# Two residual blocks gather their neighbours by indirect transfers with an add, instead of by multiplying with a neighbour matrix

## The chip, the cores and the metric

The kernel runs on one core of one Trainium2 chip. The metric is the device time of one execution in microseconds (us). Engines are named as in the profile: PE is TensorE, DVE is VectorE, ACT is ScalarE, POOL is GpSimd, and SP is the queue that issues the plain DMA transfers. PEld is the loading of weights into TensorE. Each engine works through its own instructions in the order in which they stand in the program, and waits for the others through semaphores.

## The reference, cut to what matters

There are B = 4 independent batches. For each, a mixture of low-rank experts (L0) and a cross-attention with a layer norm (L1) give `points`, 256 channels by 512 points. Then come two layers (L2 and L3) of four residual blocks each, eight blocks per batch and 32 in all. They run one after the other within a batch:

```python
idx = top_k(-squared_distance(xyz), 8)            # 8 nearest of 512 points, once per batch
for i in range(4):                                # in L2, and again in L3
    shortcut = points                             # (256 channels, 512 points)
    p = where(points >= 0, points, 0.01 * points)
    g = p gathered at idx                         # 8 neighbours of each point
    c = w_center[i] @ p
    gn = w_neighbor[i] @ g
    points = (c + gn.sum(over the 8 neighbours)) / 9 + shortcut
```

Both weights are the same matrix W here, so a block needs W p once, and then for each point the sum of nine columns of it: its own and those of its eight neighbours. The neighbours depend on `ctx_4096` alone, so a batch has one list of them for all its blocks.

## The kernel before, in words

Arrays lie with 128 partitions. A batch's x is two tiles of 128 channels by 512 points.

**A residual block** is `block(b, i)`. DVE makes p (L857). PE multiplies it with W in two halves of 256 points; this gives (W p) transposed, points on the partitions, in PSUM tiles `wp` (L869). The gather is a second product: `nbr[b, m]` is a matrix of zeros and ones that says which points are neighbours of which, with the identity added. As ones and zeros are exact in PE's shorter float format but W p is not, ACT writes a rounded copy `wph` (L882), DVE the rest `wpl` (L885), and both are multiplied by `nbr` into the two PSUM tiles `blk` (L900), 16 products of 128x128 by 128x512 in a block. DVE divides by 9 and adds x (L912). The next block of this batch needs that x, so within a batch the blocks are one chain, and PE is kept at work by changing between batches.

**What goes ahead of the blocks in a batch**: `mixture` (L392 to L489; `upd` at L448 reads the weights `lora_BT`), `values`, `queries` and `attention` (L632 to L844), with a layer norm that ends in two POOL instructions (L843 and L844), and `nearest`, which finds the eight neighbours with DVE's `max` and `match_replace` (L532, L535), makes `near` on ACT, and turns it on PE (L556) into `nbr`.

**The order** is not written by hand. `Plan.add` records each operation with an engine and a written cost; `Plan.emit` then walks through time with these costs, takes on each engine the operation that can start first, and among those that can start within 0.05 us of it the one with the lowest rank. The rank is the batch's due time from `DEADLINES` less the length of the chain that hangs on the operation. What comes out is one fixed order per engine.

Of the kernel before, what the change touches and what calls it, by code (L numbers as in the profile page):

```python
# [8 lines left out]
F32 = mybir.dt.float32  # L9
# [15 lines left out]
NL = S // 128  # L25
NBLK = 4
KNN = 8
# [1 line left out]
SLOPE = 0.01  # L29
LN_EPS = 1e-5  # L30
LOW = -3.0e38
DEADLINES = (0.0, 5.0, 15.0, 20.0)

# [2 lines left out]


EARLY = {"PE": 0.0, "ACT": 0.09, "DVE": 0.08, "POOL": 0.02, "SP": 0.0}  # L40
WARM = 20
LANES = 8
RATE = 0.3
# [16 lines left out]
class Plan:  # L60
# [5 lines left out]

    def __init__(self, places, make):
        self.places = {k: [(0.0, i) for i in range(n)] for k, n in places.items()}  # L70
        self.make, self.ops, self.wrote, self.read = make, [], {}, {}
        self.batch, self.unit, self.landed = 0, None, [0.0] * LANES

    def add(self, eng, cost, fn, ins=(), outs=(), rank=None, load=0.0, port=None):
        op = Op()
        op.port = eng == "POOL" if port is None else port
        op.eng, op.cost, op.fn, op.rank, op.load = eng, cost, fn, rank, load
        op.batch, op.unit, op.n, op.before, op.after, op.end = self.batch, self.unit, len(self.ops), set(), [], None
        for k in ins:
            if k in self.wrote:  # L80
                op.before.add(self.wrote[k])
            self.read.setdefault(k, []).append(op)
        for k in outs:
            op.before.update(self.read.pop(k, []))
            if k in self.wrote:
                op.before.add(self.wrote[k])
            self.wrote[k] = op
        op.before.discard(op)
        op.bufs = [k for k in dict.fromkeys([*ins, *outs]) if isinstance(k, Buf)]
        for k in op.bufs:  # L90
            k.users.append(op)
        for o in op.before:
            o.after.append(op)
        self.ops.append(op)

    def emit(self, deadline):
        longest = {}
        for op in reversed(self.ops):
            op.tail = op.cost + max(
                [o.tail + (SEEN[op.eng] if o.eng != op.eng else 0.0) for o in op.after if o.batch == op.batch],  # L100
                default=0.0,
            )
            if op.unit:
                longest[op.unit] = max(longest.get(op.unit, 0.0), op.tail)
            op.todo = len(op.before)
            for k in op.bufs:
                k.left = len(k.users)
        for op in self.ops:
            if op.rank is None:
                op.rank = deadline[op.batch] - longest.get(op.unit, op.tail)  # L110
        free, port = dict.fromkeys(SEEN, 0.0), {"POOL": 0.0, "DVE": 0.0}
        ready = [op for op in self.ops if not op.todo]
        while ready:
            best = {}
            for op in ready:
                t = free[op.eng] if not op.load else max(free[op.eng], self.landed[-LANES])
                if op.port:
                    t = max(t, port["DVE"] + 0.06 if op.eng == "POOL" else port["POOL"])
                t = max([t] + [o.end + (SEEN[o.eng] if o.eng != op.eng else 0.0) for o in op.before])
                want = {}  # L120
                for k in op.bufs:
                    if k.tile is None:
                        for kind in k.kinds:
                            want[kind] = want.get(kind, 0) + 1
                if any(len(self.places[kind]) < n for kind, n in want.items()):
                    continue
                for kind, n in want.items():
                    t = max(t, sorted(self.places[kind])[n - 1][0])
                best.setdefault(op.eng, []).append((t, op))
            choice = []  # L130
            for eng, found in best.items():
                first = min(t for t, _ in found)
                t, op = min((f for f in found if f[0] <= first + 0.05), key=lambda f: (f[1].rank, f[1].n))
                choice.append((t, op.n, op))
            t, _, op = min(choice)
            ready.remove(op)
            for k in op.bufs:
                if k.tile is None:
                    k.held = []
                    for kind in k.kinds:  # L140
                        self.places[kind].sort()
                        k.held.append(self.places[kind].pop(0)[1])
                    k.tile = self.make(k.kinds[0], k.held[0], k.name)
            op.fn()
            op.end = t + op.cost
            free[op.eng] = op.end - (EARLY[op.eng] if op.cost > 0.3 else 0.0)
            if op.port:
                port[op.eng] = free[op.eng]
            if op.load:
                op.end = max(op.end + 1.4, self.landed[-1]) + op.load / RATE  # L150
# [14 lines left out]
def xattn_seq_kernel(ctx: ExitStack, tc: tile.TileContext, a: dict, out: bass.AP):  # L165
# [5 lines left out]
    work = ctx.enter_context(tc.tile_pool(name="work", bufs=1))  # L171
    small = ctx.enter_context(tc.tile_pool(name="small", bufs=1))
    psum = ctx.enter_context(tc.tile_pool(name="psum", bufs=1, space=bass.MemoryType.PSUM))
    ctx.enter_context(tc.manual_schedule())

    shapes = {
# [5 lines left out]
        "full": (work, [128, 2, H], F32, 4),  # L182
        "wp": (work, [128, 2 * S], F32R, 8),
        "near": (work, [128, H], BF16, 5),
        "odd": (work, [128, H], U8, 2),
        "small": (small, [128, 4 * NB], F32, 12),
    }
# [17 lines left out]
    csq = [keep.tile([128, H], F32R, name=f"csq{b}") for b in range(B)]  # L205
    cxx = [keep.tile([128, H], F32, name=f"cxx{b}") for b in range(B)]
    WkT = [keep.tile([128, H], F32, name=f"WkT{c}") for c in range(NC)]
    nbr = {}
    nbr_tag = [
        [f"nbr0_{k}" for k in range(4)],  # L210
        [f"WkT{k}" for k in range(4)],
# [29 lines left out]

    mbias = const.tile([128, B, V], BF16, name="mbias")
    some = const.tile([128, B], F32, name="some")


    loads = []
# [22 lines left out]
    def load_points(b):  # L269
# [39 lines left out]
        rank=-1e4,  # L309
# [26 lines left out]
        ("hsel",),  # L336
        ("hsel2",),
    )
    pool(0.1, lambda: G_.memset(eps, LN_EPS), (), ("eps",), port=False)
    pool(0.1, lambda: G_.memset(above, 1.0 + LOW * 2.0**-123), (), ("above",), port=False)  # L340
    for k in range(2):
# [90 lines left out]
    def mix(b, l, zb):  # L432
# [11 lines left out]
        for h in range(2):  # L444
            pe(
                1.73,
                lambda h=h: [
                    T_.matmul(  # L448
                        ps2.tile,
                        lhsT=zT.tile[:, bass.ts(c, 128)],  # L450
                        rhs=w["lora_BT"][:, c, :],
                        start=(c == 0),
                        stop=(c == NC - 1),
                    )
                    for c in (2 * h, 2 * h + 1)
                ],
                (zT, "lora_BT"),
                (ps2,),
            )
        key = ("x", b, l)  # L460
        dve(
# [30 lines left out]
    def nearest(b):  # L492
# [36 lines left out]
        for j in range(H // 128):  # L529
# [16 lines left out]
                (near,),  # L546
            )
            nears.append(near)
        for k in range(H // 128):

            ps = Buf("bank", f"nbrT{b}_{k}", "stage")
# [297 lines left out]


    def block(b, i):
        pt, wi = x1[b], fT[:, i % NBLK]
        p = Buf("full", f"p{b}_{i}")
        for l in range(NL):
            dve(
# [3 lines left out]
                (("p", b, l),),  # L859
                port=True,  # L860
            )
        parts = []
        for m2 in range(2):
            ps = Buf("bank", f"wp{b}_{i}_{m2}")
            hi, lo = Buf("wp", f"wph{b}_{i}_{m2}"), Buf("wp", f"wpl{b}_{i}_{m2}")
            pe(
                1.73,
                lambda ps=ps, m2=m2: [
                    T_.matmul(  # L869
                        ps.tile[:, bass.ts(k, S)],  # L870
                        lhsT=p.tile[:, c, bass.ts(2 * m2 + k, 128)],
                        rhs=wi[:, c, :],
                        start=(c == 0),
                        stop=(c == NL - 1),
                    )
                    for k in range(2)
                    for c in range(NL)
                ],
                (("p", b, 0), ("p", b, 1), p, "fT"),
                (ps, hi, lo),  # L880
            )
            act(0.59, lambda ps=ps, hi=hi: A_.copy(hi.tile, ps.tile), (ps,), (hi,))  # L882
            dve(
                0.69,
# [9 lines left out]
        for m2 in range(2):  # L894
            for o in range(NL):
# [10 lines left out]
                            )  # L906

                pe(0.92, gather, (*parts[m2], ("nbr", b, 2 * m2), ("nbr", b, 2 * m2 + 1)), (pb[o],))
        for o in range(NL):
            dve(  # L910
                0.69,
# [80 lines left out]
```

## Time and profile before

| what | value |
|---|---|
| median of 3 runs | 406.25 us (405.9 to 406.34) |
| the profiled execution's own time | 406.27 us |
| its span in the profile | 404.5 us, so 1.8 us lie around the span |
| PE busy | 398.3 us, 98% of the span |
| DVE, ACT, POOL busy | 264.7, 130.4 and 93.0 us |
| granted TensorE clock | 0.998 of full speed |

The span is what the profile covers, from the first to the last thing that it records. A group of instructions in the profile stands for one source line, engine, operation and shape; it has the busy time, the mean of one, and how long the engine sat idle just before. Matmuls overlap each other in PE's pipeline, so the mean of one record is longer than what one adds to the time; what a run of them takes is read from the chain, where each piece has a start and a length.

### The profile page before, as it was taken

How to read it: one execution, taken by the hardware profiler on the slowest of the kernel's cores; microseconds unless marked ns; L12 is line 12 of the kernel's file. 1: busy time of each engine (PE TensorE's matmuls, PEld its weight loads, DVE VectorE, ACT ScalarE, POOL GpSimd, SP SyncE). 2: the span in 40 equal slices, each digit the busy share in tenths (PEclk: the TensorE clock that was granted, in tenths of full speed). 3: DMA queues.
4: the chain of work that ended last, by engine and by line, in shares of the span. 5: the costliest groups of instructions: out<-in, count | busy, mean ns of one | idle time of the engine just before them, and what ended most of it. 6: DMA issues, size and time to landing. Idle time of an engine off the chain costs nothing.

```text
span 404.5 us, 5757 instructions
## 1 busy us (share of the span) xinstructions
PE 398.3 (98%) x2324; PEld 306.6 (76%) x2324; DVE 264.7 (65%) x476; ACT 130.4 (32%) x234; POOL 93.0 (23%) x94
## 2 busy tenths in 40 slices
PE   8999999999999999999999999999999999999996
PEld 6755786656857767866778888888888888888884
DVE  3855659997999999745588644646455463635433
ACT  4652153555464485131244222111111111111110
POOL 4644320727945808605000000000000000000000
PEclk9999999999999999999999999999999999999999
DMA  6995100000000000000000000000000000010102
GB/s 229 364 421 210 52 2 0 2 2 0 2 2 0 2 2 1 2 2 0 0 0 2 0 2 0 0 2 0 2 0 1 2 0 0 2 52 1 53 0 104
DMA packets 4746, 15.33 MB, mean 38 GB/s; under 512 B 688, under 2 KB 816, under 8 KB 4080
## 3 DMA queue, kind: packets, MB, share of 16 engines
q1 hardware_dynamic: 4720, 14.97, 9.9%
q8 instruction: 18, 0.29, 0.3%
q14 instruction: 8, 0.07, 0.1%
HBM read 12.87 MB, written 2.10 MB: 37 GB/s over the span
## 4 chain that ended last, share of the span: by engine, by line
PE 98%; DVE 1%; ACT 0%; issue 0%
PE blk L900 29%; PE wp L869 27%; PE upd L448 7%; PE o L818 7%; PE q L670 7%; PE pT L786 3%; PE d L512 3%; PE avT L798 2%; PE v L632 2%; PE route L392 2%; PE s L711 2%; PE kT L578 2%; PE d L525 1%; PE zT L438 1%; PE nbrT L556 1%; PE x1T L477 1%
## 5 line engine op out<-in xcount | busy, mean ns | idle before, releaser
L869 PE MATMUL wp<-fT,p 128*128 128x256 f32 x512 | 119.0, 380 | 0.0
L900 PE MATMUL blk<-nbr,wph 128*128 128x512 f32 x256 | 109.8, 429 | 0.0
L869 PEld LDWEIGHTS wp<-fT,p 128*128 128x128 f32 x512 | 96.6, 189 | 16.8 <-issue 1.2
L900 PE MATMUL blk<-nbr,wpl 128*128 128x512 f32 x256 | 100.6, 393 | 0.9 <-DVE wpl L885 0.9
L912 DVE SCALAR_TENSOR_TENSOR x<-blk,x 128x512 f32<-128x512 f32 x64 | 43.8, 687 | 76.9 <-PE blk L900 76.9
L882 ACT CAST wph<-wp 128x512 fp32r<-128x512 f32 x64 | 37.6, 587 | 168.4 <-PE wp L869 168.4
L885 DVE TENSOR_TENSOR wpl<-wp,wph 128x512 fp32r<-128x512 f32 x64 | 44.0, 687 | 24.5 <-ACT wph L882 24.5
L900 PEld LDWEIGHTS blk<-nbr,wpl 128*128 128x128 f32 x256 | 48.2, 188 | 11.4 <-DVE wpl L885 1.6
L900 PEld LDWEIGHTS blk<-nbr,wph 128*128 128x128 f32 x256 | 48.2, 188 | 11.3 <-ACT wph L882 0.8
L857 DVE SCALAR_TENSOR_TENSOR p<-x 128x512 f32<-128x512 f32 x64 | 44.8, 732 | 0.4
L774 POOL TENSOR_TENSOR s<-s,rden 128x512 f32<-128x512 f32 x32 | 35.1, 1132 | 36.4 <-DVE rden L764 35.6
L818 PE MATMUL o<-WoT,avTs 128*128 128x512 f32 x64 | 29.6, 597 | 0.0
L448 PE MATMUL upd<-lora_BT,zTs 128*128 128x512 f32 x64 | 29.2, 600 | 0.0
L670 PE MATMUL q<-x1T,WqT 128*128 128x256 f32 x128 | 28.7, 380 | 0.0
L670 PEld LDWEIGHTS q<-x1T,WqT 128*128 128x128 f32 x128 | 23.9, 190 | 3.5 <-issue 0.5
L737 DVE TENSOR_REDUCE mx<-s 128x8 f32<-128x512 f32 x32 | 19.9, 684 | 4.9 <-PE s L711 4.8
L448 PEld LDWEIGHTS upd<-lora_BT,zTs 128*128 128x128 f32 x64 | 11.6, 190 | 12.5 <-issue 11.8
L743 DVE TENSOR_TENSOR s<-s,mx 128x512 f32<-128x512 f32 x32 | 20.1, 684 | 0.0
L752 DVE TENSOR_REDUCE den<-s 128x8 f32<-128x512 f32 x32 | 19.9, 679 | 0.2
L818 PEld LDWEIGHTS o<-WoT,avTs 128*128 128x128 f32 x64 | 11.4, 190 | 10.6 <-issue 10.4
L749 ACT ACTIVATE s<-s 128x512 f32<-128x512 f32 x32 | 18.8, 633 | 1.8 <-DVE s L743 1.6
L791 ACT COPY pTs<-pT 128x512 f32<-128x512 f32 x32 | 17.0, 597 | 7.1 <-PE pT L786 7.1
(97 smaller groups left out, 376.7 us busy)
## 6 DMA issues: line engine op xcount, KB each, us to landing
xT<-in_xT SPq DMA_DIRECT2D x4, 512.0 KB, 6.7
x<-in_x SPq DMA_DIRECT2D x4, 512.0 KB, 12.2
out<-x SPq DMA_DIRECT2D x8, 256.0 KB, 2.0
WkT<-in_WkT SPq DMA_DIRECT2D x4, 256.0 KB, 7.7
lora_BT<-in_lora_BT SPq DMA_DIRECT2D x1, 1024.0 KB, 7.9
WqT<-in_WqT SPq DMA_DIRECT2D x1, 1024.0 KB, 9.9
WvT<-in_WvT SPq DMA_DIRECT2D x1, 1024.0 KB, 11.0
rows<-in_rows SPq DMA_DIRECT2D x2, 512.0 KB, 12.0
```

What stands on the lines that cost most here:

```text
L448: T_.matmul(ps2.tile, lhsT=zT.tile[:, bass.ts(c, 128)], rhs=w["lora_BT"][:, c, :], start=(c == 0), stop=(c == NC - 1),)
L670: T_.matmul(ps.tile[:, 0:S], lhsT=w["WqT"][:, c, bass.ts(o, 128)], rhs=x1T[b].tile[:, c, :], start=(c == 0), stop=(c == NC - 1),)
L737: lambda mx=mx, ps=ps: V_.tensor_reduce(mx.tile[:, 0:HPC], heads(ps), AX.X, ALU.max),
L743: lambda mx=mx, ps=ps, s=s: V_.tensor_tensor(heads(s), heads(ps), mx.tile[:, 0:HPC].unsqueeze(2).to_broadcast([128, HPC, V]), ALU.subtract),
L774: lambda s=s, g=g: G_.tensor_tensor(heads(s), heads(s), rden.tile[:, bass.ts(g, HPC)].unsqueeze(2).to_broadcast([128, HPC, V]), ALU.mult,),
L818: T_.matmul(po.tile, lhsT=avT.tile[:, bass.ts(c, 128)], rhs=w["WoT"][:, c, :], start=(c == 0), stop=(c == NC - 1),)
L857: lambda l=l: V_.scalar_tensor_tensor(p.tile[:, l], pt[:, l], SLOPE, pt[:, l], ALU.mult, ALU.max),
L869: T_.matmul(ps.tile[:, bass.ts(k, S)], lhsT=p.tile[:, c, bass.ts(2 * m2 + k, 128)], rhs=wi[:, c, :], start=(c == 0), stop=(c == NL - 1),)
L882: act(0.59, lambda ps=ps, hi=hi: A_.copy(hi.tile, ps.tile), (ps,), (hi,))
L885: lambda ps=ps, hi=hi, lo=lo: V_.tensor_tensor(lo.tile, ps.tile, hi.tile.bitcast(F32), ALU.subtract),
L900: T_.matmul(pb[o].tile, lhsT=part.tile[:, bass.ds(m % 2 * S + o * 128, 128)], rhs=nbr[b, m], start=(m == 0 and k == 0), stop=(m == H // 12 ...
L912: lambda o=o: V_.scalar_tensor_tensor(pt[:, o], pb[o].tile, 1.0 / (KNN + 1.0), pt[:, o], ALU.mult, ALU.add),
```

## The change

In blocks 3 and 5 of batch 3 (`APART`) the gather isn't a product any more. W p goes by ACT to an SBUF tile `sums` (points on partitions, in place of `lora_BT`, which is dead by then), and from there by one plain transfer of 512 KB to a DRAM tile `rows`. Then 32 indirect transfers are issued from POOL: for each of the eight neighbours k and each of the four groups t of 128 points, one transfer fetches 128 rows of 1 KB from `rows`, chosen by the list `listed`, and adds them to the rows of `sums` where they lie. Those of one group form a chain of eight, each waiting for the one before; four chains go side by side. At the end PE turns `sums` back in 8 transposes, and DVE adds it to x as before. In these blocks the copies `wph` and `wpl` go.

For the list, batch 3's `nearest` gets, four times, a POOL product of `near` with the numbers 1 to 512, a DVE `max` that pulls the eight numbers out, and a DVE subtraction of 1. The numbers are made once by POOL (`iota` and a copy).

The planner learns of a transfer's landing by a new term `late`, its tie window of 0.05 us goes, and the due times are others. So the whole order is planned anew.

```diff
-DEADLINES = (0.0, 5.0, 15.0, 20.0)
+DEADLINES = (20.0, 24.0, 40.0, 35.0)
+APART = ((3, 3), (3, 5))
...
-                t, op = min((f for f in found if f[0] <= first + 0.05), key=lambda f: (f[1].rank, f[1].n))
+                t, op = min((f for f in found if f[0] <= first), key=lambda f: (f[1].rank, f[1].n))
...
-            op.end = t + op.cost
-            free[op.eng] = op.end - (EARLY[op.eng] if op.cost > 0.3 else 0.0)
+            op.end = t + op.cost + op.late
+            free[op.eng] = t + op.cost - (EARLY[op.eng] if op.cost > 0.3 else 0.0)
...
+            if b in listed:
+                which, best = Buf("half", f"which{b}_{j}"), Buf("small", f"best{b}_{j}")
+                pool(1.3, lambda ...: G_.tensor_tensor(which.tile, near.tile, count, ALU.mult), (near, "count"), (which,))
+                dve(0.69, lambda ...: V_.max(best.tile[:, 0:KNN], which.tile), (which,), (best,))
+                dve(0.16, lambda ...: V_.tensor_scalar(listed[b][:, bass.ts(j, KNN)], best.tile[:, 0:KNN], -1.0, None, ALU.add), (best,), (("listed", b, j),))
...
+        if (b, i) in APART:
+            return apart(b, i, p)
...
+    def apart(b, i, p):
+        rows, tiles, n = Buf("rows", f"rows{b}_{i}"), range(H // 128), APART.index((b, i))
+        gone = [("upd", k, l, h) for k in range(B) for l in range(NL) for h in range(2)]
+        def total():
+            if not sums:
+                sums.append(keep.tile([128, 2, H // 128, S], F32, tag="lora_BT", name="sums"))
+            return sums[0][:, n % 2]
+        for m2 in range(2):
+            ps = Buf("bank", f"wp{b}_{i}_{m2}")
+            product(b, i, p, m2, ps, ())
+            act(0.59, lambda ps=ps, m2=m2: A_.copy(total()[:, 2 * m2 : 2 * m2 + 2, :].rearrange("p k o -> p (k o)"), ps.tile),
+                (ps, *gone), (("sum", n % 2, m2), *(("sum", n % 2, m2, k) for k in range(2))))
+        plan.add("SP", 0.45, lambda: S_.dma_start(out=rows.tile.rearrange("(t p) o -> p t o", p=128), in_=total()),
+            (("sum", n % 2, 0), ("sum", n % 2, 1)),
+            (rows, *(("sum", n % 2, t // 2, t % 2) for t in tiles)), late=4.5)
+        for k in range(KNN):
+            for t in tiles:
+                pool(1.2,
+                    lambda k=k, t=t: G_.indirect_dma_start(
+                        out=total()[:, t, :], out_offset=None, in_=rows.tile,
+                        in_offset=bass.IndirectOffsetOnAxis(ap=listed[b][:, t * KNN + k : t * KNN + k + 1], axis=0),
+                        compute_op=ALU.add),
+                    (rows, ("listed", b, t)), (("sum", n % 2, t // 2, t % 2),), port=False, late=3.0)
+        pb = [Buf("bank", f"blk{b}_{i}_{o}") for o in range(NL)]
+        for o in range(NL):
+            pe(0.48,
+                lambda o=o: [T_.transpose(pb[o].tile[:, bass.ts(t, 128)], total()[:, t, bass.ts(o, 128)], ident) for t in tiles],
+                ("ident", *(("sum", n % 2, t // 2, t % 2) for t in tiles)), (pb[o],))
+        update(b, i, pb)
```

`product` and `update` are the old product (L869) and the old last step (L912), made into functions.

More of the change, by code (lines that the diff above doesn't have):

```diff
@@ L72, in __init__, with add @@
         self.batch, self.unit, self.landed = 0, None, [0.0] * LANES
-    def add(self, eng, cost, fn, ins=(), outs=(), rank=None, load=0.0, port=None):
+    def add(self, eng, cost, fn, ins=(), outs=(), rank=None, load=0.0, port=None, late=0.0):
         op = Op()
+        op.late = late
         op.port = eng == "POOL" if port is None else port
@@ L98, in emit @@
         for op in reversed(self.ops):
-            op.tail = op.cost + max(
+            op.tail = op.cost + op.late + max(
                 [o.tail + (SEEN[op.eng] if o.eng != op.eng else 0.0) for o in op.after if o.batch == op.batch],
@@ L173, in xattn_seq_kernel @@
     psum = ctx.enter_context(tc.tile_pool(name="psum", bufs=1, space=bass.MemoryType.PSUM))
+    dram = ctx.enter_context(tc.tile_pool(name="dram", bufs=1, space=bass.MemoryType.DRAM))
     ctx.enter_context(tc.manual_schedule())
@@ L184, in xattn_seq_kernel @@
         "near": (work, [128, H], BF16, 5),
+        "rows": (dram, [H, S], F32, 1),
         "odd": (work, [128, H], U8, 2),
@@ L207, in xattn_seq_kernel @@
     WkT = [keep.tile([128, H], F32, name=f"WkT{c}") for c in range(NC)]
-    nbr = {}
+    nbr, sums = {}, []
     nbr_tag = [
@@ L243, in xattn_seq_kernel @@
     some = const.tile([128, B], F32, name="some")
+    count = const.tile([128, H], F32, name="count")
+    listed = {b: const.tile([128, H // 128 * KNN], I32, name=f"listed{b}") for b in {b for b, _ in APART}}
     loads = []
@@ L338, in xattn_seq_kernel @@
     )
+    steps = Buf("half", "steps")
+    pool(
+        0.7,
+        lambda: G_.iota(steps.tile.bitcast(I32), pattern=[[1, H]], base=1, channel_multiplier=0),
+        (),
+        (steps,),
+        port=False,
+    )
+    pool(0.6, lambda: G_.tensor_copy(count, steps.tile.bitcast(I32)), (steps,), ("count",))
     pool(0.1, lambda: G_.memset(eps, LN_EPS), (), ("eps",), port=False)
@@ L457, in mix @@
                 (zT, "lora_BT"),
-                (ps2,),
+                (ps2, ("upd", b, l, h)),
             )
@@ L548, in nearest @@
             nears.append(near)
+            if b in listed:
+                which, best = Buf("half", f"which{b}_{j}"), Buf("small", f"best{b}_{j}")
+                pool(
+                    1.3,
+                    lambda near=near, which=which: G_.tensor_tensor(which.tile, near.tile, count, ALU.mult),
+                    (near, "count"),
+                    (which,),
+                )
+                dve(0.69, lambda which=which, best=best: V_.max(best.tile[:, 0:KNN], which.tile), (which,), (best,))
+                dve(
+                    0.16,
+                    lambda best=best, j=j: V_.tensor_scalar(
+                        listed[b][:, bass.ts(j, KNN)], best.tile[:, 0:KNN], -1.0, None, ALU.add
+                    ),
+                    (best,),
+                    (("listed", b, j),),
+                )
         for k in range(H // 128):
@@ L851, in block @@
     def block(b, i):
-        pt, wi = x1[b], fT[:, i % NBLK]
+        pt = x1[b]
         p = Buf("full", f"p{b}_{i}")
@@ L865, in block @@
             hi, lo = Buf("wp", f"wph{b}_{i}_{m2}"), Buf("wp", f"wpl{b}_{i}_{m2}")
[L866 to L881, printed above, removed]
+            product(b, i, p, m2, ps, (hi, lo))
             act(0.59, lambda ps=ps, hi=hi: A_.copy(hi.tile, ps.tile), (ps,), (hi,))
@@ L908, in block, with product @@
                 pe(0.92, gather, (*parts[m2], ("nbr", b, 2 * m2), ("nbr", b, 2 * m2 + 1)), (pb[o],))
+        update(b, i, pb)
+    def product(b, i, p, m2, ps, outs):
+        pe(
+            1.73,
+            lambda: [
+                T_.matmul(
+                    ps.tile[:, bass.ts(k, S)],
+                    lhsT=p.tile[:, c, bass.ts(2 * m2 + k, 128)],
+                    rhs=fT[:, i % NBLK, c, :],
+                    start=(c == 0),
+                    stop=(c == NL - 1),
+                )
+                for k in range(2)
+                for c in range(NL)
+            ],
+            (("p", b, 0), ("p", b, 1), p, "fT"),
+            (ps, *outs),
+        )
@@ new lines, in apart @@
+    def apart(b, i, p):
[8 more added lines that the diff above has]
+            product(b, i, p, m2, ps, ())
+            act(
+                0.59,
+                lambda ps=ps, m2=m2: A_.copy(
+                    total()[:, 2 * m2 : 2 * m2 + 2, :].rearrange("p k o -> p (k o)"), ps.tile
+                ),
+                (ps, *gone),
+                (("sum", n % 2, m2), *(("sum", n % 2, m2, k) for k in range(2))),
+            )
+        plan.add(
+            "SP",
+            0.45,
+            lambda: S_.dma_start(out=rows.tile.rearrange("(t p) o -> p t o", p=128), in_=total()),
+            (("sum", n % 2, 0), ("sum", n % 2, 1)),
+            (rows, *(("sum", n % 2, t // 2, t % 2) for t in tiles)),
+            late=4.5,
+        )
+        for k in range(KNN):
+            for t in tiles:
+                pool(
+                    1.2,
+                    lambda k=k, t=t: G_.indirect_dma_start(
+                        out=total()[:, t, :],
+                        out_offset=None,
+                        in_=rows.tile,
+                        in_offset=bass.IndirectOffsetOnAxis(ap=listed[b][:, t * KNN + k : t * KNN + k + 1], axis=0),
+                        compute_op=ALU.add,
+                    ),
+                    (rows, ("listed", b, t)),
+                    (("sum", n % 2, t // 2, t % 2),),
+                    port=False,
+                    late=3.0,
+                )
+        pb = [Buf("bank", f"blk{b}_{i}_{o}") for o in range(NL)]
+        for o in range(NL):
+            pe(
+                0.48,
+                lambda o=o: [
+                    T_.transpose(pb[o].tile[:, bass.ts(t, 128)], total()[:, t, bass.ts(o, 128)], ident)
+                    for t in tiles
+                ],
+                ("ident", *(("sum", n % 2, t // 2, t % 2) for t in tiles)),
+                (pb[o],),
+            )
+        update(b, i, pb)
@@ L909, in block, with update @@
+    def update(b, i, pb):
+        pt = x1[b]
         for o in range(NL):
```

## The prediction

> **What bounds the kernel now.** I read the page's first two parts, then the chain of waits in order of time, then the groups by shape, then windows.
>
> ```profile
> PE 398.3 (98%) x2324; PEld 306.6 (76%) x2324; DVE 264.7 (65%) x476; ACT 130.4 (32%) x234; POOL 93.0 (23%) x94
> PEclk9999999999999999999999999999999999999999
> POOL 4644320727945808605000000000000000000000
> ```
>
> PE has no free time and runs at full clock; POOL has nothing to do in the second half. The chain (start, length, work) shows what a block costs PE:
>
> ```profile
> 359.39 1.73 PE wp L869 x8
> 361.12 1.86 PE blk L900 x8
> 362.98 1.73 PE wp L869 x8
> 364.70 1.85 PE blk L900 x8
> ...
> 97.85 1.31 PE pT L786 x12
> ...
> 396.92 3.74 PE blk L900 x16
> 400.66 0.02 issue
> 400.69 0.69 DVE x L912
> ```
>
> From 275 us to 400.7 it is wp and blk end to end with no gap: a block is 2 x 1.73 for W p and 2 x 1.855 = 3.71 for the gather, 7.17 in all. Here the time is PE's work, so PE work taken out comes off the time, if what replaces it is never waited for. Transposes of this kind (128x128) take 1.31/12 = 0.109 each.
>
> ```profile
> 0.00:40.00 40.00, 38.90 (x203) 25.53 (x204) 23.00 (x57) 19.31 (x35) 19.89 (x33) 1.00 0.82 310
> 80.00:120.00 40.00, 39.67 (x373) 26.37 (x372) 37.45 (x67) 22.09 (x40) 24.62 (x21) 1.00 0.01 2
> 120.00:160.00 40.00, 39.10 (x326) 28.55 (x325) 38.45 (x70) 23.24 (x42) 20.91 (x19) 1.00 0.00 1
> 280.00:320.00 40.00, 40.00 (x180) 33.73 (x179) 22.42 (x36) 6.46 (x11) 0.00 (x0) 1.00 0.00 1
> ```
>
> The columns after the length are PE, PEld, DVE, ACT, POOL, clock, DMA share and GB/s. From 80 to 160 us DVE is nearly as full as PE (37.5 and 38.5 of 40): attention is where DVE could become the bound. From 280 on it is half idle.
>
> **What is removed.** Two gathers, 2 x 3.71 = 7.42 of PE, put back as 2 x 8 transposes, 16 x 0.109 = 1.74. Net 5.7 off PE. Also 4 DVE subtractions go (L885, 0.687 each, 2.7). ACT keeps its four copies: another destination, the same 0.59.
>
> **What is added, beside PE.** POOL: four products `which` (as L471, 1.37 each) and the numbers, some 7 in all; DVE: four `max` of 0.69 and four small ones of 0.16, 3.4. They run in the first 60 us, before DVE is full: by 10 us slices DVE idles 25 of the first 60 us. The four `which` stand in POOL's listing between the additions L471 and L489 of batches 0 and 1, each of which can be held 1.4; PE has other batches' work there, so I count nothing; without that cover the worst is 4 x 1.4 = 5.6.
>
> **The transfers.** Before has no transfer issued by POOL and none that adds. Three prices are needed.
> - Plain, 512 KB to DRAM: the nearest row is the output's 256 KB,
>
> ```profile
> out<-x SPq DMA_DIRECT2D x8, 256.0 KB, 2.0
> cxx<-in_ctx SPq DMA_DIRECT2D x5, 128.0 KB, 4.2
> ```
>
> 2.0 to landing; another 256 KB at the 418 GB/s that this trace reaches is 0.6. I take 2.6, between 2.0 and the 4.5 that the planner writes. Its issue on SP is 0.33 (L922); SP has only this and outputs left to do then.
> - Landing of an indirect transfer of 128 KB, L: from 2.0 (that row) to 4.2 (128 KB among crowded loads). The Trainium skill (DMA: Bandwidth & Descriptors, Anatomy of one DMA) gives 2.0 + bytes/436e3 for a transfer that GpSimd issues, an estimate of 2.3 here; an add also reads its destination. I take 2.6.
> - Issue on POOL, I: from 0.33 (what SP's issue takes[...]) to where POOL would do nothing else until the landing, 2.3. An ordinary POOL instruction on a 128x512 tile is 1.13 to 1.38. I take 1.15, near those rows. The planner writes 1.2; for PE its written costs are what the trace shows (1.73, 0.92, 0.59 against 1.73, 0.93, 0.587), but no row vouches for this one.
>
> Four transfers are in flight, so a round of four takes the longer of 4 I and I + L: 4.6 or 3.75. Issue decides; L sets the round from 3.45 on, and at 4.2 eight rounds would take the 43 us of cover found below.
>
> **Is it covered?** PE works in its listed order, so if the transposes come up before the last add has landed, everything behind them waits. In the changed listing, between (3,3)'s second wp and its transposes stand 11 wp groups of 1.73, 19 half gathers of 0.93, 4 pieces of `o` of 1.73, 2 avT of 1.0, 4 pT of 0.44 and one nbrT of 0.4: 47.7 of PE work. Between (3,5)'s wp and its transposes: 13 wp and 28 half gathers, 48.5. From this go ACT's copy with its hand-overs (1.2), SP's issue and landing (2.9) and the last hand-over (0.2): 43.4 and 44.2 are left for 32 I + L. With my values that is 32 x 1.15 + 2.6 = 39.4: covered by 4.0 and 4.8. The limit is I = 1.27.
> Each transfer adds to bytes that the one four before it wrote, so POOL waits for that landing in place; behind POOL's 32 issues in (3,3) stand batch 2's last layer norm instructions, four of 1.3 (L843, L844). The first block of batch 2 is listed 60 us of PE work after (3,3)'s wp; less 4.1 to the first issue, 5.3 of POOL, 1.5 of DVE for p and 0.8 of hand-overs, 48.6 are left, so it is late only from I = 1.5. The transposes are late first.
>
> **A rule that speaks against it.** L857, 128x512, is 0.73 on average, and in the window from 275 to 401 us 0.684:[...] only instructions like L469, 0.525, run faster. The Trainium skill (SBUF — State Buffer, Who interferes with whom) says that POOL and DVE share a port pair: a DVE instruction in a two-port mode locks POOL out, so that it can't write descriptors, and one with two SBUF inputs contends with POOL's reads. If p (L857, both inputs in SBUF, 1.4 to 1.5 per 7.17 of blocks, 20%) held POOL's descriptor work up, I would be 1.15/0.8 = 1.44 and 32 I + L = 48.7: late by 5.3 and 4.5, so 411. If only the fast mode does, just the layer norm's L838 (0.82, twice) is in the way, 1.6 at most, inside the 4.0 of slack: 401. I take the second, as descriptor work writes rather than reads, but keep the first for the range.
>
> **The new order.** Nothing in the first 150 us stays in place: attention of batches 0, 1 and 3 is now ahead of all blocks, and the nearest neighbours of batches 2 and 3 move up into the first 60 us. I added up the durations of DVE's work that must be done ahead of each matmul that waits for it, against PE's work listed ahead of that matmul. Between 60 and 140 us PE's sum leads by 10 or more before and by 3.8 at the least after, at batch 3's second scores. DVE's own idle time sits in that lead (28 us by then in before), and the work moved up (8 `max`, 8 `match_replace` of 0.68, and 3.4 for the list, 14.4 in all) falls where that idle time is. If all of it fits, nothing is lost; if none, the lead lost, 10 - 3.8 = 6.1, is PE waiting. On the other side PE idles only 398.3 + 1.1 (start) + 3.8 (end) against 404.5, so a better order could win 1.3. Value 0.7, ends -1.3 and 6.1.
> The end is as before: two batches in turn, which from 360 us on shows no gap.
>
> **The sum**, against the profiled execution's 406.27 (median of the runs 406.25, the same): 406.3 - 5.7 + 0.7 = 401.3.
>
> **The rivals.**
> - *Covered (A)*: 401.3; with the ends of the order and a slack of a few us, 399.3 to 405.
> - *PE waits at the transposes (B), slower.* One mechanism: POOL's issue of an indirect transfer costs more than 1.27, and PE, in its order, stands at (3,3)'s and (3,5)'s transposes. Each 0.1 on I is 3.2 per block. The saving is gone at stalls of 5.0, at I = (43.8 + 2.5 - 2.6)/32 = 1.37. At 1.4 it is 401.3 + 4.0 + 3.2 = 408.5, at 1.5 it is 414.9, at 1.6 about 421. For it: no slack to speak of between the planner's places and the price it writes, no row of an issue, and the rule above. Against: ordinary POOL rows under 1.4, and an idle DMA system then (0.00 share).
> - *The new order eats it (C)*: DVE falls behind in attention and PE waits up to 6.1: 406.3 - 5.7 + 6.1 = 406.7. For it: DVE at 38 of 40 us; against: 28 us of idle time ahead of it.
> - *It doesn't do what it says*: if the four chains were in truth one, each transfer waiting for the one before, it would be 32 (I + L) = 120, 76 late in each block: some 550. The listing shows each issue waiting for the one four before, so I leave this out.
>
> **How the numbers follow.** A 0.56, B 0.32, C 0.12. About 0.2% (0.8 us) is what a measurement of this kernel can tell from no change. A is faster throughout; C spreads over 404.5 to 406.7 and gives 0.02 faster, 0.06 same, 0.04 slower; B is slower but for its edge. Faster 0.58, same 0.06, slower 0.36. The prediction is A's 401.3. The range starts at 399.0, below A's end, and reaches to 415, B with I = 1.5; what lies above is B's tail, about 0.12. Cases of both signs hold much of the chance: A alone is 399.3 to 405.
>
> **What would show it.** Right: blk at two places replaced by 8 transposes with no PE idle before them; POOL's 32 issues of one block within 38 us; from (3,5) on, wp and blk end to end; a PE end near 395.7. Wrong: PE idle ahead of the transposes in a row whose releaser is a DMA (B, its length is 32 I + L - 43.4, which gives I); rows of `issue` or DVE waits on PE between 60 and 160 us that sum to over 3 (C); 128 KB landings over 4.2, which makes the round latency's and not issue's.

## The result, and the profile after

| | before | after |
|---|---|---|
| median | 406.29 us (4 runs, 405.9 to 406.55) | 447.98 us (4 runs, 447.57 to 448.49) |
| ratio, 95% interval | | 1.1024 (1.1009 to 1.104) |
| span of the profiled execution | 404.5 us | 445.9 us |
| mean granted clock | 0.998 | 0.954 |
| end of PE's last matmul | 400.7 us | 442.0 us |

The changed kernel is slower by 10%, 41.7 us. The first parts of its page:

```profile
PE 400.9 (90%) x2308; PEld 307.5 (69%) x2308; DVE 269.7 (60%) x480; ACT 129.2 (29%) x234; POOL 197.5 (44%) x164
PE   8999999989979999999999950899999419999996
PEclk9999999998999999999999985699999858999999
POOL 5633450635618960430388888404888860000000
```

PE has two holes, at about 60% and about 80% of the span, and each falls at the end of a stretch in which POOL is busy. In each hole and just after it the granted clock is low. Two groups of the page name both sides:

```profile
L985 POOL DMA_INDIRECT sums<-rows,listed x64 | 100.0, 1563 | 64.4 <-DMA rows<-sums 23.3
L1002 PE MATMUL blk<-ident,sums 128*128 128x128 f32 x16 | 5.5, 445 | 33.0 <-DMA sums<-rows,listed 33.0
```

L985 is the transfers' issue on POOL, L1002 the transposes: PE sat idle 33.0 us ahead of these 16 instructions, and what ended the waits was the landing of the last adds. How far apart POOL's issues are is read from its timeline (start, length, then the idle time before it):

```profile
263.99 1.55 POOL L985 DMA_INDIRECT sums<-rows,listed  x1 [0.30 <-issue]
265.84 1.54 POOL L985 DMA_INDIRECT sums<-rows,listed  x1 [0.30 <-issue]
...
275.09 1.54 POOL L985 DMA_INDIRECT sums<-rows,listed  x1 [0.30 <-issue]
276.94 1.55 POOL L985 DMA_INDIRECT sums<-rows,listed  x1 [0.30 <-issue]
```

From the start of one issue to the start of the next it is 1.85 us: 1.55 busy and 0.30 in which POOL waits for nothing that the profile shows. The end of the chain of waits, at the first hole and at the end:

```profile
276.64 0.30 issue
276.94 3.72 DMA sums<-rows,listed
280.66 0.04 issue
280.70 1.33 PE blk L1002 x5
282.03 1.71 PE blk L921 x4
283.74 2.73 PE wp L936 x8
...
438.27 3.74 PE blk L921 x16
442.03 0.69 DVE x L1015
```

The last transfer starts on POOL at 276.94 and has landed at 280.66, and only then does PE go on. (`wp` x8 takes 2.73 there, and took 1.73 before: the clock.) PE's other waits are shorter:

```profile
PE blk L1002 <- DMA sums<-rows,listed: 33.0, 8, 12.9
PE pT L820 <- DVE s L777: 2.4, 2, 1.9
PE x1T L494 <- ACT pTs L825: 1.7, 2, 1.5
PE wp L936 <- DVE s L777: 1.0, 1, 1.0
```

The kernel before had no wait of PE on `s` or for `x1T`; its PE waits are 1.1 at the start, 0.9 and 0.3. These are losses of the new order in the first 220 us. The 1.5 us at `x1T` is put down to ACT's `pTs`, but `pTs` was done at 98.26, and PE went on at 99.13, when DVE's first copy into `x` had just ended:

```profile
98.31 1.33 DVE L490 COPY_PREDICATED x<-odd,hi 128x512 f32<-128x512 uint8 x2
```

So most of these waits are for DVE. Windows give their sum, and the clock around the first of them and behind the holes (length, then PE, PEld, DVE, ACT, POOL busy, clock, DMA share, GB/s):

```profile
0.00:100.00 100.00, 95.81 (x644) 65.32 (x645) 78.62 (x168) 47.51 (x90) 42.80 (x55) 1.00 0.35 130
100.00:220.00 120.00, 116.05 (x824) 87.34 (x823) 91.78 (x158) 50.09 (x91) 50.91 (x43) 0.99 0.02 5
...
90.00:100.00 10.00, 7.96 (x96) 4.68 (x95) 10.00 (x17) 4.62 (x10) 3.18 (x4) 1.00 0.01 2
180.00:190.00 10.00, 8.98 (x69) 7.59 (x62) 10.00 (x18) 4.32 (x8) 3.34 (x3) 1.00 0.00 0
...
97.90:101.30 3.40, 1.60 (x11) 1.22 (x12) 3.40 (x6) 1.35 (x3) 1.46 (x2) 1.00 0.00 0
101.30:104.70 3.40, 3.40 (x13) 2.95 (x12) 3.40 (x8) 2.82 (x6) 1.04 (x1) 0.50 0.00 0
280.70:285.60 4.90, 4.90 (x14) 4.14 (x15) 4.22 (x6) 0.00 (x0) 2.75 (x3) 0.50 0.00 0
368.20:371.00 2.80, 2.79 (x9) 2.45 (x10) 1.98 (x3) 0.00 (x0) 0.00 (x0) 0.50 0.00 0
```

In the first 220 us PE idles 220 - 95.81 - 116.05 = 8.1, against 2.3 before: 5.8 more. Where it waits from 90 to 100 and from 180 to 190, DVE is busy all the time (before, from 90 to 100, DVE was busy 8.16 and PE 10.00). At 101.3 us comes a step of 3.4 us at half the clock, which costs 1.7. Behind the two holes the clock is at half for 4.9 and 2.8 us more, 3.9 lost.

So the 41.3 us by which PE ends later are made up of: 5.7 saved; 18.1 and 17.1 lost at the two sets of transposes (262.14 to 280.70 and 350.69 to 368.21, less 0.44, the length of one transpose, in each); 3.9 of slow clock behind them; and 7.5 of the order, 5.8 + 1.7. The sum is -5.7 + 35.2 + 3.9 + 7.5 = 40.9, and 0.4 have no place. The 35.2 is more than the row's 33.0, as in each hole three transposes ran one by one between the waits, 0.44 to 0.48 each.

### The profile page after: what moved, and what is told of

It reads as the page before. It is cut to its first block, busy times and chain, and to the rows that moved or that the text cites. A ratio compares the mean times of both kernels' runs of the same rounds, so it can differ in the third digit from the quotient of the medians.

```text
span 445.9 us, 5842 instructions
## 1 busy us (share of the span) xinstructions
PE 400.9 (90%) x2308; PEld 307.5 (69%) x2308; DVE 269.7 (60%) x480; ACT 129.2 (29%) x234; POOL 197.5 (44%) x164
## 3 DMA queue, kind: packets, MB, share of 16 engines
q0 software_dynamic: 9216, 8.39, 13.5%
## 4 chain that ended last, share of the span: by engine, by line
PE 36%; POOL 20%; DVE 6%; issue 5%; DMA 2%; ACT 1%; POOLq 0%; ACTq 0%
POOL sums L985 20%; PE blk L921 15%; PE wp L936 14%; PE o L852 3%; DMA sums<-rows,listed 2%; DVE p L891 2%; PE pT L820 2%; DVE mx L771 1%; PE avT L832 1%; PE q L704 1%; DVE x L1015 1%; DVE s L777 1%; DVE wpl L906 1%; PE blk L1002 1%; PE v L666 0%
## 5 line engine op out<-in xcount | busy, mean ns | idle before, releaser
L985 POOL DMA_INDIRECT sums<-rows,listed x64 | 100.0, 1563 | 64.4 <-DMA rows<-sums 23.3
L921 PE MATMUL blk<-nbr,wph 128*128 128x512 f32 x240 | 103.7, 432 | 0.0
L921 PE MATMUL blk<-nbr,wpl 128*128 128x512 f32 x240 | 95.3, 397 | 0.0
L903 ACT CAST wph<-wp 128x512 fp32r<-128x512 f32 x60 | 35.0, 585 | 192.9 <-PE wp L936 192.9
L906 DVE TENSOR_TENSOR wpl<-wp,wph 128x512 fp32r<-128x512 f32 x60 | 41.2, 689 | 72.1 <-ACT wph L903 72.0
L921 PEld LDWEIGHTS blk<-nbr,wph 128*128 128x128 f32 x240 | 46.0, 192 | 10.1 <-issue 0.2
L921 PEld LDWEIGHTS blk<-nbr,wpl 128*128 128x128 f32 x240 | 45.8, 191 | 9.9 <-issue 0.2
L891 DVE SCALAR_TENSOR_TENSOR p<-x 128x512 f32<-128x512 f32 x64 | 47.1, 766 | 4.4 <-POOL x L878 3.8
L1002 PE MATMUL blk<-ident,sums 128*128 128x128 f32 x16 | 5.5, 445 | 33.0 <-DMA sums<-rows,listed 33.0
L1002 PEld LDWEIGHTS blk<-ident,sums 128*128 128x128 f32 x16 | 3.0, 206 | 35.5 <-issue 25.7
```

The lines of the kernel that those rows point to most:

```text
L891: lambda l=l: V_.scalar_tensor_tensor(p.tile[:, l], pt[:, l], SLOPE, pt[:, l], ALU.mult, ALU.max),
L906: lambda ps=ps, hi=hi, lo=lo: V_.tensor_tensor(lo.tile, ps.tile, hi.tile.bitcast(F32), ALU.subtract),
L921: T_.matmul(pb[o].tile, lhsT=part.tile[:, bass.ds(m % 2 * S + o * 128, 128)], rhs=nbr[b, m], start=(m == 0 and k == 0), stop=(m == H // 12 ...
L985: lambda k=k, t=t: G_.indirect_dma_start(out=total()[:, t, :], out_offset=None, in_=rows.tile, in_offset=bass.IndirectOffsetOnAxis(ap=list ...
```

## The experiments

The theory after the result: the transfers' issue on POOL alone makes the 35.2 and the slow clock behind it, and the order makes the rest. The rivals: the transfers cost something else too (a landing, the bytes, a port), or the multiplications' saving was never there. The runs with fewer, changed or no transfers leave neighbours out of the sum or add wrong rows, so they say something of the time alone. All medians stand beside runs of the kernel before on the same chip (406.31 for the first four, 406.44 for the last four).

**Half of the issues.**

```diff
-                    lambda k=k, t=t: G_.indirect_dma_start(
+                    lambda k=k, t=t: k < KNN // 2 and G_.indirect_dma_start(
```

> Only the first four of the eight neighbours are fetched and added in the two blocks (the other 16 transfers of each are left out, so four neighbours are missing from the sum); the planner still counts 32, so the order of everything else is that of the changed kernel. Theory 1 (each issue holds POOL for 1.85 us, and PE waits for the last of 32): 16 x 1.85 + 2.2 = 31.8 is less than the 43.4 us of PE work listed between product and transposes, so PE's 35 us of waiting go, and with them the slow clock after them (4): 408 to 410 us. What is left above 406.3 - 5.7 = 400.6 is then the price of the new order alone, some 8. Theory 2 (the new order, attention crowded ahead of the blocks, is most of the loss): over 430.

Measured: 413.13 us (410.74 to 413.51, 5 runs), ratio 1.0156 (1.0115 to 1.0198). The wait at the transposes is gone, with the issue still at 1.85. So the number of issues on POOL sets that wait. But 413 is 3 to 5 above what this theory left over. The trace, of the fastest of the five (410.74), has a wait that was not in the changed kernel's list, and a long pair of `p` just ahead of it:

```profile
PE blk L921 <- DVE wpl L906: 2.5, 1, 2.5
...
248.60 5.35 DVE L891 SCALAR_TENSOR_TENSOR p<-x 128x512 f32<-128x512 f32 x2
```

The other four (412.69 to 413.51) ran at a lower mean clock, 0.985 to 0.992 against 0.994. What they waited for is not on record.

**The planner told the true prices.**

```diff
-            late=4.5,
+            late=3.6,
...
-                    1.2,
+                    1.85,
...
-                    late=3.0,
+                    late=2.1,
```

> The planner's written costs of the transfers are set to what the trace of the changed kernel shows: 1.85 for an issue (was 1.2), 2.1 to its landing (was 3.0), 3.6 for the plain transfer (was 4.5). All 32 transfers of each block stay. Theory 1: the planner lists enough PE work ahead of the transposes, the waiting goes, and the same early order leaves its 8 us: 408 to 410, slower than before the change by 2 to 4. Rival (the issue costs PE something else too, such as slower PE or DVE work beside 64 x 1.85 us of POOL): over 412. Rival (the early loss was chance of that one order): 401 to 404.

Measured: 414.14 us (413.81 to 414.58, 4 runs), ratio 1.0181 (1.014 to 1.0222). All 64 transfers run, PE never waits for one, and 34 us are won back by three numbers in the planner. Again it ends above what was expected, where the first rival was set (over 412). The chain shows where:

```profile
278.00 1.24 DVE x L1015 x2
279.24 6.56 DVE p L891 x2
285.80 0.61 DVE wpl L906
286.41 0.04 issue
286.46 2.52 PE blk L921 x7
```

Two `p` take 6.56 us here; elsewhere two take 1.3. What POOL does beside them, from its timeline:

```profile
279.08 3.12 POOL L877 TENSOR_TENSOR x<-x,rows 128x512 f32<-128x512 f32 x2
281.57 3.07 POOL L878 TENSOR_TENSOR x<-x,rows 128x512 f32<-128x512 f32 x2
```

These are the last four layer-norm instructions of batch 2, which stand behind the 32 issues on POOL. They came to run exactly when DVE reached `p`. Two runs below test whether they are the cause.

**No add.** The line `compute_op=ALU.add` is left out, so each transfer overwrites.

> The transfers copy instead of adding, so the sum is left out and only the last neighbour's row stays; order, waits, sizes are those of the changed kernel. Theory 1 (what POOL does is write descriptors, and those are as many with or without the add): issue to issue stays 1.85 (1.75 to 1.9), time 446 to 448.5; the landing may be 0.1 to 0.5 shorter. Rival (the add is what is dear): issue to issue under 1.5, and 10 us or more less waiting in each block.

Measured: 409.11 us in one run, and the issue is cheaper:

```profile
L985 POOL DMA_INDIRECT sums<-rows,listed x64 | 61.9, 967 | 62.7 <-ACT pTs L825 22.2
```

It is 0.95 busy and 0.30 between, 1.25 from start to start. The expectation that the add costs POOL nothing failed, and its rival came: of the 1.85, the add is 0.60. At 1.25 PE doesn't wait at the transposes, as the prediction's limit of 1.27 would have it; the landing is shorter too, 2.7 from the start of an issue.

**64 rows instead of 128 in each transfer**, with the add.

```diff
-                        out=total()[:, t, :],
+                        out=total()[0:64, t, :],
...
-                        in_offset=bass.IndirectOffsetOnAxis(ap=listed[b][:, t * KNN + k : t * KNN + k + 1], axis=0),
+                        in_offset=bass.IndirectOffsetOnAxis(ap=listed[b][0:64, t * KNN + k : t * KNN + k + 1], axis=0),
```

> Each transfer fetches and adds the rows of 64 partitions only (the other 64 points of each group get no neighbours). Number of transfers, chain and order are the same. If an issue's cost is per row: 0.3 + 1.54 x 64/128 = 1.07, so 32 x 1.07 + 2.2 = 36.4, all covered, 408 to 410. If it is a fixed price per transfer: 1.85 and 448. In between (a fixed part of about 1 and the rest per row): 1.45, 5 us of waiting in each block, 420.

Measured: 439.76 us in one run, none of the three values expected; the issue is 1.71 from start to start, 0.14 less for half of the rows.

```profile
L1002 PE MATMUL blk<-ident,sums 128*128 128x128 f32 x16 | 5.5, 445 | 24.4 <-DMA sums<-rows,listed 24.4
```

The wait row falls by 33.0 - 24.4 = 8.6, against 2 x 32 x 0.14 = 9.0 from the issue alone. So most of the price belongs to the transfer, not to its rows: two points give 1.57 + 0.0022 per row.

**The changed order with no transfer at all.**

```diff
-                    lambda k=k, t=t: G_.indirect_dma_start(
+                    lambda k=k, t=t: k < 0 and G_.indirect_dma_start(
```

> The changed kernel with its order unaltered and none of the 64 indirect transfers issued (the two blocks then lack their neighbours' rows; W p itself is still copied, stored and transposed). Theory: what is left is the order and the multiplications saved. Order: PE sat idle 2.0 + 0.5 + 2.3 + 1.0 us in the first 220 us of the changed kernel and ran about 1.7 us slower at the clock's dip near 101 us, 7.5 to 7.7 together; saved 5.7. So 406.3 + 7.6 - 5.7 = 408.2, 407.5 to 409.5, and DVE's p near 250 to 280 us does not stretch. Rival: the order itself costs all that the half count and the true-price order lost against it (413 to 414), through p waiting for batch 2's layer norm on POOL whatever POOL did before: then 412 or more, with a p of 5 to 6 us in it.

Measured: 408.36 us (407.53 to 408.93, 4 runs), ratio 1.0052 (1.0035 to 1.0069), and the longest `p` is 1.76. The order and the saving alone leave the kernel 1.9 slower than before. PE's early waits are all still there, without a transfer in the program:

```profile
PE pT L820 <- DVE s L777: 2.2, 2, 1.9
PE x1T L494 <- ACT pTs L825: 1.7, 2, 1.5
PE wp L936 <- DVE s L777: 1.0, 1, 1.0
```

**The four layer-norm instructions moved to DVE**, in the kernel with the true prices.

```diff
-        pool(1.35, lambda: G_.tensor_tensor(y, y, rows["ln_g"], ALU.mult), ("rows2",), (key,))
-        pool(1.35, lambda: G_.tensor_tensor(y, y, rows["ln_b"], ALU.add), ("rows2",), (key,))
+        pool(1.35, lambda: (V_ if b == 2 else G_).tensor_tensor(y, y, rows["ln_g"], ALU.mult), ("rows2",), (key,))
+        pool(1.35, lambda: (V_ if b == 2 else G_).tensor_tensor(y, y, rows["ln_b"], ALU.add), ("rows2",), (key,))
```

> The kernel planned with the true prices, with the four last layer-norm instructions of batch 2 (the multiply and the add of its two halves) run by DVE at their place in the order instead of POOL. Theory: in that kernel the two p instructions at 279 us took 6.6 us instead of 1.3 because POOL's four layer-norm instructions ran beside them (279.1 to 284.6 us); PE then waited 3.3 us for wpl and ran at half its clock for one step of 3.4 us, 1.7 us more. Without them on POOL both go, and DVE's four instructions cost 2.8 us on an engine with idle time there: 414.1 - 5.0 = 409.1, 408 to 410.5; no p above 1.5 us. Rival: p stretches because of POOL's transfers (their descriptors are written then as well), not its arithmetic: a p of 5 us or more stays, and 413 to 415.

Measured: 408.57 us (407.62 to 408.98, 4 runs), ratio 1.005 (1.0032 to 1.0067), 5.6 below the kernel that it changes, and the longest `p` is 1.75 (up to 1.5 was expected; the run with no transfer has one of 1.76). With all 64 transfers in it, it is as fast as the run with none (408.36; the intervals lie on each other). So transfers that are covered cost PE nothing that these runs can tell. In the kernel with the true prices, what the layer norm on POOL cost is read from the trace: PE's wait of 3.3 for `wpl` and 1.7 for one step at half the clock behind it, 5.0 in all. That trace also has a slow step at 130 us which this run's has not, and which has nothing to do with the layer norm. In the run with half of the issues the same pair of `p` ran beside the same four POOL instructions; that these were its excess was not tested apart.

**The early order of the kernel before.** The operations up to POOL's last arithmetic are emitted in a listed order, that of the kernel before; the rest is planned with the due times of the kernel before, and the two blocks belong to two batches.

```diff
-DEADLINES = (20.0, 24.0, 40.0, 35.0)
+DEADLINES = (0.0, 5.0, 15.0, 20.0)
-APART = ((3, 3), (3, 5))
+APART = ((2, 1), (3, 6))
...
+        turn = list(reversed(FIRST))
         while ready:
             best = {}
-            for op in ready:
+            for op in [o for o in ready if o.key is None or o.key == turn[-1]] if turn else ready:
...
-                    1.2,
+                    1.9,
...
-                    late=3.0,
+                    late=2.2,
```

> Two blocks of different batches go by transfers, (2,1) and (3,6), with 1.9 us per transfer and 2.2 us behind each in the planner. All of the work up to the last arithmetic of POOL (190 us) is emitted in exactly the order of the kernel before, and only what follows is planned anew, with the due times of the kernel before; the lists of neighbours are made at 200 to 220 us. Theory: each of the three losses was one of order, not of the transfers: no idle time of PE at 90 to 130 us, no layer norm on POOL beside p, no wait at the transposes as 62 us of other PE work lies under each set. Then only the saving is left, 5.7, less up to 0.8 for idle time near 210 us: 400.6 to 401.5, faster than the kernel before by 1.2 to 1.4 per cent. Rival: transfers cost something that follows them into any order (PE or DVE slowed while POOL issues, or a clock dip at the hand-over): then 404 or more.

Measured: 401.91 us (401.8 to 402.3, 4 runs), ratio 0.9892 (0.9875 to 0.9908): faster than both kernels. It ends 0.4 above the range expected. Lines of its page, and behind them PE's waits (all but the one of 1.1 at the start):

```profile
PE 393.1 (98%) x2308; PEld 302.1 (76%) x2308; DVE 270.9 (68%) x488; ACT 130.0 (32%) x234; POOL 205.4 (51%) x168
PEclk9999999999999999999999999999999999999999
L1000 POOL DMA_INDIRECT sums<-rows,listed x64 | 101.6, 1587 | 49.5 <-issue 25.7
```

```profile
PE blk L936 <- DVE wpl L921: 0.9, 2, 0.5
PE wp L951 <- DVE p L906: 0.6, 1, 0.6
PE pT L835 <- ACT pTs L840: 0.3, 1, 0.3
```

POOL spends as long on the 64 issues as in the changed kernel, and nothing waits for it. PE is busy 5.2 less than before, and of what is left over 0.6 is one new wait, at the `p` near 212 us, which takes 2.25 for two while POOL makes the last products for the list. Blocks, lists and order were all changed at once here, so the run shows that the saving can be had, not which of these won how much.

**Plain transfers with the add, without the list.**

```diff
-                    lambda k=k, t=t: G_.indirect_dma_start(
+                    lambda k=k, t=t: G_.dma_start(
                         out=total()[:, t, :],
-                        out_offset=None,
-                        in_=rows.tile,
...
-                        compute_op=ALU.add,
+                        in_=rows.tile[bass.ts(t, 128), :],
+                        accum_op=ALU.add,
```

> The changed kernel with each of the 64 indirect transfers replaced by a plain transfer of POOL, of 128 consecutive rows with the same add (so it adds other rows than the neighbours'), order unaltered. It asks what the 1.57 us that does not depend on the number of rows is for. Theory 1: it is the list: POOL must read 128 indices and write a descriptor per row. Then a plain one takes at most 1.25 us in all, the stalls at the transposes go, and the time is 408 to 414. Theory 2: it is the price of a transfer with add from POOL, list or not: 1.6 us or more per transfer, PE waits 20 us or more, and 436 to 448.

Measured: 409.41 us in one run, no wait at the transposes.

```profile
230.31 5.44 POOL L985 DMA_DIRECT2D sums<-rows  x6 [0.20 <-issue]
236.11 4.67 POOL L985 DMA_DIRECT2D sums<-rows  x5 [0.36 <-DMA sums<-rows]
```

Six in 5.44 and five in 4.67 are 0.91 and 0.93 apiece. So with the add in both, the list makes about 0.9 of the 1.85. A plain transfer from POOL without add was not run, so whether the two prices simply add up is open.

## Why the prediction was wrong

The forecast was 401.3 us, with a range of 399.0 to 415.0; measured were 447.98, slower than before and 33 above the range. The case that came is the prediction's B, its mechanism and its place to the letter, with a price far past the end that was given to it. Case C came with it: its sign, waits of PE for DVE of over 3 us between 60 and 160 us, is there (3.9). C alone would have turned the forecast: the run with no transfer (408.36) is slower than before.

- **The step that failed: the issue on POOL, I.** It was set at 1.15, "near those rows" of ordinary POOL arithmetic, and measured 1.85. The 0.70 more, 64 times, are 44.8; less the 8.8 of cover that the sum had found in the two blocks, 36.0 of stall are left, and 35.2 were measured. Ordinary POOL rows are no neighbours of an issue. An indirect copy takes 1.25, near the 1.15 and the planner's 1.2, and the add puts 0.60 on top; the sum had no term for the add on POOL. The bounds of 0.33 and 2.3 held the value. But the range was closed at I = 1.5 with 0.12 of chance above it, where nothing in the trace spoke for stopping. The 1.5 had no row near it, and 0.1 of I is 6.4 us in the two blocks together.
- **The formula was right.** A stall of 32 I + L - 43.4 (and 44.2), with the measured 1.85 and a landing of 2.2 behind the busy part of the issue, gives 18.0 and 17.2; measured were 18.1 and 17.1. That they agree to 0.1 is in part luck: the last 0.30 of I is counted twice so, and some longer issues (1.77 to 2.06 busy) make up for it. The limit of I = 1.27 is supported by the run without the add, which at 1.25 did not wait.
- **The cover was right.** 47.7 of PE's work between the second `wp` of (3,3) and its transposes was read from the listing; in the trace it goes from 214.33 to 262.14, 47.8. From that `wp` to the first issue it was 4.5 instead of 4.1; the plain transfer took 3.0 instead of 2.6.
- **The rule weighed.** With p holding POOL's descriptor work up, I would have been 1.44; the other reading was taken. The trace sides with that choice: I is 1.85 at 263.99 us, where DVE stands still, and 1.85 around it where DVE works. Single issues are longer by 0.1 to 0.5. But the other half of that rule (the Trainium skill, SBUF — State Buffer, Who interferes with whom: two SBUF inputs on DVE contend with a POOL instruction that reads SBUF) was not taken into the sum, though the prediction had named the four layer-norm instructions behind the 32 issues. In the kernel after, these four run from 277.9 to 283.4, most of it inside the stall, and no `p` there takes over 1.8; take the stall away, and they cost about 5 us, which the run with DVE's layer norm shows.
- **The second step that failed: the order,** valued at 0.7 with ends of -1.3 and 6.1, cost 7.5. Waits of PE are 5.8 of it, near the far end; the 1.7 of the clock were not in any term. The run without transfers confirms the size: 408.36 - (406.44 - 5.7) = 7.6. What was weighed was DVE's sum of work against PE's over a long stretch, with idle time of DVE that lay elsewhere: from 90 to 100 us DVE has none, and PE waits for the piece that comes next in its own list. Which of the change's edits to the order (due times, the tie window, the operations for the list) makes them was not separated.
- **The slow clock was missing.** After each hole PE works at half of the clock for some us more, which costs 3.9 together; the prediction counted the stall alone.
- **The saving was right.** 5.7 was forecast; PE's busy time fell by 5.2 where nothing got in its way (393.1 against 398.3), and the time by 4.5. The case A existed, at 401.9 against the 401.3 forecast, but in an order that the changed kernel did not have.

## What to carry to other kernels

Work that is moved to an idle engine is free only up to the cover that the order leaves over it, so divide that cover by the number of instructions, and ask whether any row of the trace shows that such an instruction takes less. Where none does, measure that one price before the planner or the forecast uses it: here 0.65 us more than the planner's 1.2, 64 times, cost some 39 of the 42 us, with the slow clock behind the holes. True prices in the planner won 34 of them back; with the old early order as well it was 1.1% faster than before. And a plan that is told true prices is not done: what stands behind the long stretch on the same engine is moved too, here into the one place where it held up DVE.

## What the runs showed of the hardware that was not expected

- The issue on POOL of a transfer of 128 rows of 1 KB, from start to start: 1.85 us with list and add, 1.25 with the list alone, about 0.92 with the add alone, 1.71 with list and add for 64 rows. The profile counts 9,216 packets on this queue with list and add, as many with the add alone, and 3,072 with the list alone; so the price does not follow the packets.
- The landing was 3.6 to 4.2 us from an issue's start, and four issues take 7.4, so no issue ever waited for the one four before; with the plain ones at 0.92, POOL did wait for landings, 7.6 us in 12 places.
- PE's clock goes in steps of 3.4 us, at 1.00 or 0.50: in the kernel after, the slow stretches end at 104.7, 285.6 and 371.0 us, and these lie 53 and 25 times 3.41 us apart. The step at 101.3 us was at half though PE had been busy for 1.60 of the 3.40 us ahead of it. The Trainium skill (TensorE: Matmul & The Clock Gate, What's actually happening) has the half clock after at least one idle window of about 3.4 us; here a window that was idle for half its length was enough. Over the traces that have slow steps, outside the holes, PE had worked 1.0 to 1.7 us in the window ahead of each of eleven slow steps; two steps behind 1.55 us were not slow, and none behind 1.8 or more. The steps don't begin at the same moment in each execution (one begins at 101.3 us here and at 99.8 in the run with no transfer), so whether a gap of this size costs 1.7 us more is in part chance.
- Two `p` on DVE beside four POOL instructions took 6.56 us instead of 1.3, while POOL's four took 5.6 together, where one alone takes 1.27. DVE pays nearly all of it.
